# Two graph-attention layers on one core: VectorE in fixed order at the joint of the layers, and the first half tile's shift read from PSUM

## The chip, the cores and the metric

The kernel runs on one core of a Trainium2 chip. A core has five engines with a queue each: TensorE (PE; its weight loads are listed apart as PEld), VectorE (DVE), ScalarE (ACT), GpSimd (POOL) and SyncE (SP), which only issues transfers. The metric is the device time of one execution in microseconds; the time of a kernel is the median of its runs.

## The reference

Two layers, each with a residual, on x (2708 x 1024, float32) and a 0/1 adjacency matrix (2708 x 2708):

```
h = relu(layernorm(x))
layer 0:  f = h@Wf + bf;  g = h@Wg + bg
          e = relu(f @ g.T);   scores = where(adj > 0, e, -9e15)
          x = x + softmax(scores, axis=1) @ (h@W + bW)
h = relu(layernorm(x))
layer 1:  hh = h@W1;  f1 = hh@a1;  f2 = hh@a2
          e = leaky_relu(f1 + f2.T, 0.2);   scores = where(adj > 0, e, -9e15)
          x = x + relu(softmax(scores, axis=1) @ hh)
```

In layer 1 the scores are cheap: a column plus a row. The two vectors are computed as h@(W1@a1) and h@(W1@a2), that is, two dot products for each row of h.

## The kernel before, in words

The nodes are cut into 22 tiles of up to 128 (128 partitions) and into 5 panels of four tiles each (three panels have a few columns more). Tiles are taken in pairs; NQ = 10 pairs and one left-over unit. All large products are done by one level of Strassen's scheme (products M1 to M7, on halves); layer 1's panels 1 to 4 use two levels in the aggregation.

Layer 0 goes panel by panel: scores, softmax, `aggregate` (weights times h), `project` (times W). After `project` of a tile, `rows_done` has the new rows of x: it normalizes them into h, takes the two dot products (`dots(0)` into f[0], which is f1, `dots(1)` into f[1], which is f2) and raises the running column maximum of masked f2 for every panel (`raise_max`). `pair_h` forms Strassen sums of the pair's h (tiles g) and stores them.

The joint of the layers begins when the last panel (tiles 16 to 19, pairs 8 and 9) is projected. For a tile of that panel `rows_done` takes dots(1) at once, raises panel 0's maximum, and appends dots(0) to a list. After the last tile, `shifts1(0, make)` turns the running maximum (mx) by five TensorE transposes (mx_ps in `column_max`), reduces it to the columns mcol, and makes three small columns in some eight VectorE instructions: z, "none" and the shift m. Between the transposes and the reductions it calls `make`, the first half of `pair_h`; the second half, `rest[0]`, follows.

Then `take_weights(0)` calls `weights1(0, ...)`. For panel 0 the unnormalized scores of eight tiles were made ahead (`scores_before`, tiles P). `spread` puts the shift column along a row on all partitions: TensorE transposes into a PSUM bank sp_ps (four columns to a bank), and `copy` moves that to mb, by VectorE and ScalarE in turns. For each of the eight tiles the shift mb is then subtracted and ScalarE takes the exponential; for the others, two more spreads (of z and "none", into ub and vb) come first. `aggregate(1, 0, ...)` follows: its first product M1 reads the left half (288 columns) of the first tile, into the banks gx.

What sets the order. The program's text gives an order of tracing; a planner then orders each engine's instructions when the kernel is built. An instruction that is ready goes before one that is not; among ready ones the earlier in the program goes first. `tc.keep_in_program_order` ties an instruction behind the one traced before it on its engine. `InOrder` applies that to every instruction of the engines named in `nc.hold`; here `nc.hold` is empty. Loads by SyncE always keep program order. Deferred work stands in the list `later` with a price in us; `behind(us)` adds credit and runs entries while there is credit (in layer 1's panel 0, 4.0 at each call, four calls in a product), the loads of the first entries being issued ahead. `weights1` puts its 24 entries (2.1 each) before those already listed; running maxima for the panels 2 to 4 stand in a second list, `lazy`, which is used when `later` is empty.

All tiles named h_last, P, mb, maskl, g and most others come from one pool of 54 buffers of 128 x 576 float32; hc (rows of h for the aggregation) from a pool of 12.

Of the kernel before, what the change touches and what calls it, by code (L numbers as in the profile page):

```python
# [11 lines left out]
AF = mybir.ActivationFunctionType  # L12
# [45 lines left out]
def kernel(  # L58
# [19 lines left out]
    nc = InOrder(tc)  # L78
# [31 lines left out]
    NQ = len(pairs)  # L110
    pair_of = {t: (t // 2, t % 2) for t in range(MONO)}
    LEFT = NQ
    units = pairs + [(MONO, TINY)]
# [11 lines left out]
    def slot(name, shape=(P, WX), dt=FP):  # L125
        return slots.tile(list(shape), dt, tag="slot", name=name)
# [18 lines left out]
    def bank(name, shape=(P, W), dt=FP):  # L145
        return psum.tile(list(shape), dt, tag="bank", name=name)
# [44 lines left out]
    def copy(o, i):  # L191

        flip[0] ^= 1
        (nc.vector.tensor_copy if flip[0] else nc.scalar.copy)(o, i)
# [6 lines left out]
    def put(us, go, fetch=None, takes_psum=False, ready=None, to=later):  # L201
        to.append([us, fetch, go, takes_psum, ready])

    def one(of=None):
        of = later if of is None else of
        for it in of[:4 if of is lazy and from_slots[0] else ahead[0]]:
            if it[1]:
                it[1]()
                it[1] = None
        us, _, go = of.pop(0)[:3]  # L210
        go()
        return us

    def behind(us, psum_free=False):
# [3 lines left out]
        while spare[0] and not later and lazy and credit[0] > 0:  # L218
            credit[0] -= one(lazy)

    def flush():
        while later:
            one()
# [18 lines left out]
    def halves(t):  # L242
        return [t[:, e * W:(e + 1) * W] for e in range(2)]
# [1 line left out]
    def row_halves(name, from_stream=False):  # L245
        return halves(stream(name)) if from_stream else [slot(name)[:, :W] for _ in range(2)]

    def spread(o, cols):

        at = 0  # L250
        for g in range(0, len(cols), 4):
            ps = bank("sp_ps")
            w = 0
            for cl in cols[g:g + 4]:
                n = cl.shape[0]
                nc.tensor.transpose(ps[:, w:w + n], cl.to_broadcast([n, P]), ident[:n, :n])
                w += n
            copy(o[:, at:at + w], ps[:, :w])
            at += w

# [14 lines left out]
    def sub(o, a, b):  # L275
        nc.vector.tensor_tensor(o, a, b, OP.subtract)

    def columns_of(p, col):
        return [col[:n, i:i + 1] for i, (_, n) in enumerate(pieces[p])]
# [357 lines left out]
    for name, gs in (("pick_lo", (0, 1)), ("pick_hi", (0, 2, 3))):  # L637
        t = consts.tile([P, P], FP, name=name)
        cols = lambda g: ident[:, B32 * g:B32 * (g + 1)]
# [667 lines left out]
    f = [consts.tile([P, n], FP, name=f"f{k}") for k, n in enumerate((NCOL, NT))]  # L1307
# [204 lines left out]
    def shifts1(p, between=None):  # L1512

        k, t0 = len(pieces[p]), first_col[p]
        top = column_max(p, mx[p], between)[:, :k]
        f1 = f[0][:, t0:t0 + k]
        z, m, c, d = (stats.tile([P, 5], FP, name=nm)[:, :k] for nm in ("z", "m1", "none", "m2"))
        nc.vector.tensor_add(z, f1, top)
        nc.vector.tensor_scalar(c, top, -BIG / 2, None, op0=OP.is_ge)
        nc.vector.tensor_scalar(d, top, -BIG / 2, -BIG, op0=OP.is_lt, op1=OP.mult)  # L1520
        nc.vector.scalar_tensor_tensor(m, z, ALPHA, z, op0=OP.mult, op1=OP.max)
        nc.vector.tensor_mul(m, m, c)
        nc.vector.tensor_add(m, m, d)
        sub(z, f1, m)
        nc.vector.scalar_tensor_tensor(c, f1, ALPHA, m, op0=OP.mult, op1=OP.subtract)
        return z, c, m
# [3 lines left out]
    def rows_done(t, xt):  # L1530

        done_rows[t] = xt

        def dots(k):
            c = t if k else col_of[t]
            dot(f[k][:, c:c + 1], done_rows[t], halves(wab[k]))
            if k == 1:
                nc.vector.tensor_scalar(f2s[:, t:t + 1], f[1][:, t:t + 1], ALPHA, None, op0=OP.mult)
            elif t == MONO:
                nc.gpsimd.dma_start(f[0][:NM, HALF:HALF + 1], f[0][NM:, c:c + 1])  # L1540

        q, k = pair_of.get(t, (LEFT, t - MONO))
        mine = units[q]
        whole = all(s in done_rows for s in mine)
        if panel_of[t] == NP - 1:
            done_rows[t] = row_halves("h_last")
            normalize(xt, done_rows[t])
            if whole and q == NQ - 1:
                tc.keep_in_program_order(nc.scalar.activation(stats.tile([P, 1], FP, name="warm"), eps, AF.Exp))
            raise_it = lambda: raise_max(0, q, k, first_mask[t][:, :width[0]])  # L1550
            if not whole:
                dots(1)
                raise_later.append(raise_it)
                put(1.6, lambda: dots(0))
            else:
                raise_later.pop()()
                dots(1)
                raise_it()
                put(1.6, lambda: dots(0))
                rest = []  # L1560
                make = lambda: rest.append(pair_h(q, *(done_rows[s] for s in pairs[q])))
                if q == NQ - 1:
                    got["zm"] = shifts1(0, make)
                else:
                    make()
                rest[0]()
                put_max(1, q)
                if q == NQ - 1:
                    for m in BY_QUARTERS:
                        put_quarters(m, q // 2, later)  # L1570
                    for p in range(2, NP):
                        for s in (NQ - 2, NQ - 1):
                            put_max(p, s, lazy)
            return

        def met():
            known.add(q)
            for p in range(NP):
                if generated[p] > q:
                    put_max(p, q)  # L1580
        put(1.5, lambda: moments(xt))
        put(0.5, lambda: normalize(xt))
        put(1.6, lambda: dots(0))
        put(1.6, lambda: dots(1))
        if whole and q == LEFT:
            put(0.0, lambda: left_h(1, *(done_rows[s] for s in mine)))
            put(0.0, met)
        elif whole:
            put(2.7, lambda: pair_h(q, *(done_rows[s] for s in pairs[q])))
            put(0.0, met)  # L1590
            quads_met[q // 2] = quads_met.get(q // 2, 0) + 1
            if quads_met[q // 2] == 2:
                put(0.0, lambda: [put_quarters(m, q // 2) for m in BY_QUARTERS])
# [82 lines left out]
    got = {}  # L1676
    generated = [0] * NP
    before, spreaded = {}, []
# [27 lines left out]
    for p in range(NP):  # L1706
# [3 lines left out]
        S = got["S"]  # L1710
# [34 lines left out]
    def weights1(p, z, m, shift):  # L1745

        w = width[p]
        ub, vb1, sm = slot("ub"), slot("vb1"), slot("sm")

        def spreads():  # L1750
            spread(ub, columns_of(p, z))
            spread(vb1, columns_of(p, m))
        if p == 0:
            mb = slot("mb")
            spread(mb, columns_of(p, shift))
        else:
            spreads()
        S = [None] * NT
        order = order_of_units
        exps[0] = 0  # L1760

        def go(i, mk):
            if i < len(order):
                q, k = order[i]
                n, t = P, units[q][k]
                if p == 0 and t in before:
                    S[t] = before.pop(t)
                    s = S[t][:n, :w]
                    sub(s, s, mb[:n, :w])
                else:  # L1770
                    if p == 0 and not spreaded:
                        spreads()
                        spreaded.append(True)
                    S[t] = slot("P")
                    s = S[t][:n, :w]
                    nc.scalar.activation(s, vb1[:n, :w], AF.Identity, bias=f2s[:n, t:t + 1])
                    nc.vector.scalar_tensor_tensor(s, ub[:n, :w], f[1][:n, t:t + 1], s, op0=OP.add, op1=OP.max)
                    add(s, s, mk[0][:n, :w])
                nc.scalar.activation(s, s, AF.Exp)
            if i >= LAG:  # L1780
                q, k = order[i - LAG]
                total(p, sm, S[units[q][k]], once(q, k), i == LAG)
            exps[0] += 1

        front = []
        for i in range(len(order) + LAG):
            mk = []
            front.append([2.1, (lambda i=i, mk=mk: mk.append(load_mask(p, *order[i])))
                          if i < len(order) and not (p == 0 and units[order[i][0]][order[i][1]] in before) else None,
                          (lambda i=i, mk=mk: go(i, mk)), False, None])  # L1790
        later[:0] = front
        return S, sm
# [39 lines left out]
    for p in range(NP):  # L1832
        S, sm = got["P"]
# [5 lines left out]
        g = aggregate_quartered(p, S, sm, next_right, then, fine=1.0) if p else aggregate(1, p, S, sm, then, rate=4.0)  # L1839
# [34 lines left out]
```

## Time and profile before

| | |
|---|---|
| median of 3 runs | 3078.0 us (3077.63 to 3078.73) |
| the profiled execution | 3082.24 us, span 3080.5 us |
| TensorE busy | 3000.0 us, 97% |
| VectorE busy | 2046.6 us, 66% |
| ScalarE, GpSimd busy | 551.7 us, 505.5 us |
| last product of layer 0 ends | 2124.9 us |
| transposes of the running maximum | 2133.19 to 2134.52 us |
| transposes of the shift, z and "none" | 2138.37 to 2142.47 us |
| first product of layer 1 | 2142.53 us |

The span runs from the first to the last instruction of the program; what lies around it is in the execution's time. Times in rows are microseconds from the start of the span. Almost all VectorE and ScalarE work has line 45, a helper's, so it is told apart by the names of tiles: "mx<-maskl,f,mx" is `raise_max`, "junk<-h_last,wab" a pass of a dot product (two for each), "f<-part" the sum of the two passes, "g<-h_last" a sum of `pair_h`, "mcol<-mx_ps" a reduction, "P<-P,mb" the subtraction of the shift.

### The profile page before, as it was taken

How to read it: one execution, taken by the hardware profiler on the slowest of the kernel's cores; microseconds unless marked ns; L12 is line 12 of the kernel's file. 1: busy time of each engine (PE TensorE's matmuls, PEld its weight loads, DVE VectorE, ACT ScalarE, POOL GpSimd, SP SyncE). 2: the span in 40 equal slices, each digit the busy share in tenths (PEclk: the TensorE clock that was granted, in tenths of full speed). 3: DMA queues.
4: the chain of work that ended last, by engine and by line, in shares of the span. 5: the costliest groups of instructions: out<-in, count | busy, mean ns of one | idle time of the engine just before them, and what ended most of it. 6: DMA issues, size and time to landing. Idle time of an engine off the chain costs nothing.

```text
span 3080.5 us, 41669 instructions
## 1 busy us (share of the span) xinstructions
PE 3000.0 (97%) x14630; PEld 2301.1 (75%) x14630; DVE 2046.6 (66%) x4577; ACT 551.7 (18%) x895; POOL 505.5 (16%) x786
## 2 busy tenths in 40 slices
PE   8998999899999999999999999998999999999998
PEld 4576777657877588885888886784767959879695
DVE  5776693776661586715965276867878768787853
ACT  3420020021110121101211011302222131212200
POOL 1421101310011110214102011131202010020202
PEclk9999999999999999999999999998999999999999
DMA  6988967987565786758967588679757768878786
GB/s 220 304 259 245 302 248 251 314 285 228 177 241 146 226 262 218 247 155 240 284 206 253 165 233 275 230 292 323 250 193 266 260 203 295 289 268 297 266 293 249
DMA packets 447809, 766.80 MB, mean 249 GB/s; under 512 B 175488, under 2 KB 262304, under 8 KB 447568
## 3 DMA queue, kind: packets, MB, share of 16 engines
q1 hardware_dynamic: 392624, 598.30, 60.1%
q0 software_dynamic: 54976, 165.83, 16.1%
q8 instruction: 116, 1.90, 0.2%
q14 instruction: 93, 0.76, 0.1%
HBM read 630.04 MB, written 138.11 MB: 249 GB/s over the span
## 4 chain that ended last, share of the span: by engine, by line
PE 79%; DVE 9%; DMA 5%; issue 5%; SPq 1%; ACT 1%; POOL 0%; POOLq 0%; DVEq 0%; ACTq 0%
PE sz L1385 7%; PE gz L664 6%; PE gx L664 6%; PE gy L664 6%; PE gz L1074 5%; PE pz L1274 5%; PE sx L1385 5%; PE px L1274 4%; PE sy L1385 4%; PE py L1274 4%; PE gx L1074 3%; PE gy L1074 3%; PE gv L664 3%; PE M_ps L577 3%; PE qz L664 3%
## 5 line engine op out<-in xcount | busy, mean ns | idle before, releaser
L1385 PE MATMUL sz<-B,As 128*128 128x288 f32 (+2 forms) x1200 | 292.7, 393 | 3.4 <-DVE st L45 3.3
L1385 PEld LDWEIGHTS sz<-B,As 128*128 128x128 f32 x1200 | 228.1, 191 | 53.0 <-DVE st L45 6.8
L1385 PE MATMUL sx<-B,As 128*128 128x288 f32 (+2 forms) x800 | 203.0, 397 | 13.5 <-DMA As<-hs_d 12.0
L1385 PE MATMUL sy<-B,As 128*128 128x288 f32 (+2 forms) x800 | 199.0, 392 | 0.0
L664 PE MATMUL gz<-Sa,hc 128*128 128x288 f32 (+2 forms) x800 | 190.3, 399 | 6.3 <-DMA hc<-hg_d 6.3
L1385 PEld LDWEIGHTS sx<-B,As 128*128 128x128 f32 x800 | 153.4, 192 | 47.5 <-DMA As<-hs_d 8.0
L664 PEld LDWEIGHTS gz<-Sa,hc 128*128 128x128 f32 x800 | 154.5, 194 | 40.4 <-DMA hc<-hg_d 6.7
L1385 PEld LDWEIGHTS sy<-B,As 128*128 128x128 f32 x800 | 151.7, 190 | 30.6 <-DVE st L45 0.3
L1074 PE MATMUL gz<-quarter,hc 128*128 128x128 f32 (+2 forms) x1344 | 168.8, 279 | 3.8 <-DVE gT L45 3.7
L143 POOL DMA_DIRECT2D out_dram<-x_res x180 | 89.1, 501 | 482.0 <-DVE x_res L45 473.5
L1074 PEld LDWEIGHTS gz<-quarter,hc 128*128 128x128 f32 x1344 | 160.6, 191 | 5.1 <-DVE gT L45 4.6
L1274 PE MATMUL px<-w,gT 128*128 128x512 f32 x320 | 141.2, 593 | 1.5 <-ACT pt L45 1.5
L1274 PE MATMUL py<-w,ps 128*128 128x512 f32 x320 | 142.2, 593 | 0.0
L1274 PE MATMUL pz<-w,ps 128*128 128x512 f32 x320 | 142.1, 594 | 0.0
L143 POOL DMA_DIRECT2D mk_d<-mask x55 | 36.0, 654 | 523.7 <-DVE mask L45 517.3
L1274 PEld LDWEIGHTS pz<-w,ps 128*128 128x128 f32 x320 | 60.2, 190 | 76.2 <-issue 70.5
L1274 PEld LDWEIGHTS py<-w,ps 128*128 128x128 f32 x320 | 60.5, 190 | 75.1 <-issue 72.7
L1274 PEld LDWEIGHTS px<-w,gT 128*128 128x128 f32 x320 | 60.1, 190 | 72.9 <-issue 67.1
L577 PE MATMUL M_ps<-wgT,wfT 128*128 128x512 f32 x256 | 112.5, 595 | 1.6 <-ACT hsT L45 1.6
L664 PE MATMUL gy<-T,hc 128*128 128x288 f32 (+2 forms) x480 | 111.6, 394 | 0.0
L45 ACT ACTIVATE P<-P 128x576 f32<-128x576 f32 (+2 forms) x110 | 72.0, 655 | 207.5 <-DVE P L45 207.4
L984 POOL TENSOR_TENSOR gT<-gT,rr 128x2304 f32<-128x2304 f32 (+5 forms) x12 | 44.4, 3700 | 378.0 <-DVE rr L45 172.7
(382 smaller groups left out, 5892.1 us busy)
## 6 DMA issues: line engine op xcount, KB each, us to landing
hc<-hg_d SPq DMA_DIRECT2D x175, 512.0 KB
As<-hs_d SPq DMA_DIRECT2D x150, 512.0 KB
hc<-hr_d SPq DMA_DIRECT2D x119, 512.0 KB
hc<-hs_d SPq DMA_DIRECT2D x112, 512.0 KB
w<-wt_d SPq DMA_DIRECT2D x96, 512.0 KB
w<-in_L_gnn_W_dram SPq DMA_DIRECT2D x72, 512.0 KB
md<-md_d SPq DMA_DIRECT2D x56, 512.0 KB
adj_i<-in_adj_dram SPq DMA_DIRECT2D x200, 128.0 KB
```

What stands on the lines that cost most here:

```text
L45: i = f(*a, **k)
L143: nc.gpsimd.dma_start(a, b)
L577: nc.tensor.matmul(ps, wfT[a][c // NH][:, c % NH, :], wgT[b][c], start=(c == 0), stop=(c == NC - 1))
L664: nc.tensor.matmul(ps[d], left(m, k, d), right(m, k), start=(start and k == 0), stop=(k == K - 1), skip_group_check=True)
L984: nc.gpsimd.tensor_tensor(of(e, s), of(e, s), by(s, k), OP.mult)
L1074: nc.tensor.matmul(ps[:, d], lhs[:, d * P:(d + 1) * P], inner_right(m, n, k), start=(start and k == 0 and d == 0), stop=(k == NK - 1), ski ...
L1274: nc.tensor.matmul(ps, left[i][m][:, k, :], w_[k], start=(start and k == 0), stop=(k == NH - 1), skip_group_check=True)
L1385: nc.tensor.matmul(ps[:n, :h], lefts[q][:, i % 2, c, :n], B[m][c // 2][:, c % 2, :h], start=(start and c == 0), stop=(c == NH - 1), skip_g ...
```

## The change

- Two helpers: `held(f, ...)` runs f with VectorE's instructions tied to program order; `call` runs it plainly.
- `rows_done`, last panel: dots(0) of the tiles of pair 8 is done at once instead of being listed; that of pair 9 stays listed and is held. For pair 9 the last `raise_max`, `shifts1` with the first half of `pair_h`, and the second half are held.
- `weights1`, panel 0: the spread of the shift is held, and `sooner` is called when the first four transposes are issued: it subtracts the shift from the first half of the first tile straight from the PSUM bank and takes the exponential of that half. The first tile's entry then does the second half alone; the subtractions of the first three tiles are held.

```diff
+    def held(f, *a):
+        was, nc.hold = nc.hold, ("vector",)
+        r = f(*a)
+        nc.hold = was
+        return r
+
+    def call(f, *a):
+        return f(*a)
...
-    def spread(o, cols):
+    def spread(o, cols, sooner=None):
...
+            if sooner and g == 0:
+                sooner(ps)
             copy(o[:, at:at + w], ps[:, :w])
...
             if not whole:
                 dots(1)
                 raise_later.append(raise_it)
-                put(1.6, lambda: dots(0))
+                dots0 = lambda: dots(0)
+                if q == NQ - 1:
+                    put(1.6, lambda: held(dots0))
+                else:
+                    dots0()
             else:
+                last = q == NQ - 1
                 raise_later.pop()()
                 dots(1)
-                raise_it()
-                put(1.6, lambda: dots(0))
+                (held if last else call)(raise_it)
+                if last:
+                    put(1.6, lambda: held(dots, 0))
+                else:
+                    dots(0)
                 rest = []
                 make = lambda: rest.append(pair_h(q, *(done_rows[s] for s in pairs[q])))
-                if q == NQ - 1:
-                    got["zm"] = shifts1(0, make)
+                if last:
+                    got["zm"] = held(shifts1, 0, make)
                 else:
                     make()
-                rest[0]()
+                (held if last else call)(rest[0])
                 put_max(1, q)
...
         if p == 0:
             mb = slot("mb")
-            spread(mb, columns_of(p, shift))
+            t = units[0][0]
+
+            def sooner(ps):
+                s = before[t][:, :w // 2]
+                sub(s, s, ps[:, :w // 2])
+                nc.scalar.activation(s, s, AF.Exp)
+            held(spread, mb, columns_of(p, shift), sooner)
         else:
             spreads()
...
                 if p == 0 and t in before:
                     S[t] = before.pop(t)
-                    s = S[t][:n, :w]
-                    sub(s, s, mb[:n, :w])
+                    s = S[t][:n, (w // 2 if i == 0 else 0):w]
+                    (held if i < 3 else call)(sub, s, s, mb[:n, (w // 2 if i == 0 else 0):w])
```

## The prediction

> **What bounds the kernel now.** I read the page first, then TensorE's waits from 2075 us on, the chain, the timeline of the joint engine by engine, and SyncE's waits there. The page:
>
> ```profile
> span 3080.5 us, 41669 instructions
> PE 3000.0 (97%) x14630; PEld 2301.1 (75%) x14630; DVE 2046.6 (66%) x4577; ACT 551.7 (18%) x895; POOL 505.5 (16%) x786
> ```
>
> TensorE is busy 97% of the span, so a gain elsewhere counts only where TensorE stands still. Its waits between 2075 us and the end, longest first:
>
> ```profile
> PE mx_ps L856 <- DVE mx L45: 8.3, 1, 8.3
> PE gz L1089 <- DVE V L45: 4.6, 3, 2.2
> PE sp_ps L256 <- DVE m L45: 4.4, 2, 3.9
> ```
>
> The first row and 3.85 us of the third are the joint of the layers: TensorE ends layer 0 at 2124.9, transposes the maximum at 2133.19, the shifts at 2138.37, and starts layer 1 at 2142.53. The chain there (start, duration, work) runs through VectorE:
>
> ```profile
> 2131.06 0.60 DVE g L45
> ...
> 2131.74 0.61 DVE junk L45 x2
> ...
> 2132.41 0.72 DVE mx L45
> 2133.14 0.60 DVE g L45
> 2133.74 0.61 DVE junk L45 x2
> 2134.35 0.60 DVE g L45
> 2134.95 0.98 DVE mcol L45 x5
> 2135.94 0.60 DVE g L45
> ...
> 2136.89 0.61 DVE junk L45 x2
> ...
> 2137.59 0.64 DVE junk L45 x2
> ...
> 2142.53 21.25 PE gx L664 x80
> ```
>
> "mx" is the last running maximum, "mcol" the five reductions. "g" (sums for Strassen) and "junk" (dot products) are needed by nobody here: they were ready while the chain's next instruction was not, and then the chain waited for them. TensorE's own timeline:
>
> ```profile
> 2138.37 1.41 PE L256 MATMUL sp_ps<-ident,m 128*128 128x128 f32 x5 [3.85 <-DVE m L45]
> 2139.72 1.41 PE L256 MATMUL sp_ps<-ident,z 128*128 128x128 f32 x5
> 2141.06 1.41 PE L256 MATMUL sp_ps<-ident,none 128*128 128x128 f32 x5
> 2142.53 17.86 PE L664 MATMUL gx<-P,hc 128*128 128x288 f32 x66
> ```
>
> These 15 transposes run without a gap and end 0.06 us before the first product. So the product has two releasers that come almost together: the exponential (the chain's view) and TensorE's own three groups.
>
> **The skill.** "TensorE: Matmul & The Clock Gate", section "What's actually happening", says that the clock is halved after an idle window of about 3.4 us and returns after about 3.4 us of sustained work, on a free-running window. The trace agrees: the granted clock is 0.50 in every slice from 2130 to 2144, 1.00 from 2146; the first 80 products take 21.25 us, the next 80 19.40, so the cold start costs 1.85 us. "PSUM — Partial Sum Buffer", section "Engine vs sequencer instructions", says that VectorE's queue is strictly first in, first out and that matmuls start in program order; that is what makes fillers and transposes binding, and the timeline shows nothing against it. "VectorE: DVE Perf Modes", section "Why PSUM operands drop a tier", says that fp32 operands in PSUM run at the base rate; here a 128x288 subtraction takes 459 ns from SBUF (T<-P) and 435 to 458 ns for an addition from PSUM (m<-gy, gT<-gy), so reading PSUM costs nothing extra.
>
> **Part 1: the dots of tiles 16 and 17 are traced at once.** Each is two 0.61 us passes and a small sum, 2.6 us for both tiles. They leave the joint, where they were fillers, and land between 2101 and 2112. VectorE idles there (0.88 at 2104.6, 1.65 at 2112.1, 3.27 at 2116.4), so they are absorbed before 2119.7. At most they delay the eviction of py at 2110.20 by about 2.6 us, to 2113.5; its bank is needed at 2114.4. Cost zero; without the cover, under 1 us.
>
> **Part 2: the last maximum.** Before, one g and one junk pass lie between the accumulator read (end 2131.06) and mx (2132.33). With the sums and the dots of tiles 18 and 19 held behind, nothing ready is left; the scalar f, its scaled copy and mx follow with waits of about 0.04 us between dependent instructions (as at 2123.55 and 2123.75): f 2131.10, copy 2131.28, mx 2131.36. Gain 0.97; mx ends 2132.17.
>
> **Part 3: maximum to reductions.** Before: g, junk, g, 1.81 us. After: the two held sums, the second dependent on the first: 0.61 + 0.72 = 1.33; the transposes need about 1.15 beside them. Gain 0.48.
>
> **Part 4: reductions to the shift.** The g at 2135.94 (0.60) moves behind the small instructions. The two junk passes and the f between them (0.61 + 0.07 + 0.64) go too; the small instructions, which overlap them now, then show their own latency, about 0.3. Gain 0.60 + 1.32 - 0.3 = 1.6. Parts 2 to 4 give 3.0: the shifts' transposes start at 2135.4 in place of 2138.37.
>
> **Part 5: the first half straight from PSUM.** After the shift VectorE issues the last two sums (1.3 us) beside the first four transposes (1.1), then a 128x288 subtraction (0.45) and ScalarE an exponential (0.40 as for the 128x288 copy m<-qx): ready about 2.3 us after the transposes start. It takes the full copy (0.60), half a subtraction (0.30) and half an exponential (0.29) off that branch, 1.2 us. But the other two groups of transposes stand before the product in the program, they are ready at once, and 15 of them last 4.1 us at the half clock. So the branch has 1.8 us of slack and this part gives only the 0.06. The second half costs one more small instruction on VectorE and on ScalarE, under 0.2 us, beside two products of TensorE (over 3 us cold).
>
> **Part 6: dots of tiles 18 and 19.** They move behind the weights, 2.6 us of VectorE near 2190 to 2197. That queue is full until 2205 (39.90 of 40 us from 2165 to 2205), but starts 3 us earlier and has lost two dot passes (2140.4, 2151.9). The next TensorE needs there, sums for the product at 2205 and the bank of gy (2224), were done by 2193 and 2196. Cost zero; without the cover at most 2.6.
>
> **Part 7: what moves in the queues.** The list of deferred work loses two entries of 1.6 us. With 4.0 us of credit at each call, the first four mask loads of the later panels' maxima are then issued before, not after, the first two loads of the third-next product (M6, first used 2205.25). And four buffers (h_last of tiles 18 and 19) stay taken from about 2141 or 2152 until about 2195. SyncE is a queue in order and does wait for such buffers:
>
> ```profile
> SPq L139 <- DVE P L45: 22.2, 5, 11.7
> SPq L139 <- DVE junk L45: 12.4, 2, 8.4
> ```
>
> Before, M6's first two loads were issued by 2168.1 and six masks then held the queue from there to 2195.3. Behind the masks, M6's loads would be issued near 2192 (3 us earlier, as VectorE's work is) and land some 5 us later (estimate from 3.9 for a 256 KB load of the same tensor and 5.4 for a 512 KB store to it): 2197 against a need at 2202. Hidden, with 5 us of cover instead of over 30.
>
> **Sum.** 0.97 + 0.48 + 1.6 + 0.06 = 3.1, less about 0.1 for the extra small instructions: 3.0. The clock's phase can move this: before, the product started just after a window began and was cold for 3.2 us; another phase costs up to one window more, 1.7 us, or saves a few tenths. I take zero, since the runs shown contain such phases too. TensorE is busy nearly without a break afterwards (368.3 of 385 us from 2095 to 2480; of the 16.7 missing, 12.1 lie between 2125 and 2143), so the 3.0 carries to the end. The profiled execution took 3082.24 (span 3080.5); this would make its span 3077.5. The median of the runs, 3078.0, lies 4.2 lower than the profiled execution; I subtract the same difference: **3075.0 us**.
>
> **Rivals.** 0.2% of the time is 6.2 us; a measurement of this kernel can hardly tell less from no change, so a move from 3071.8 to 3084.2 is "same".
>
> B, the product goes ahead of the two other groups of transposes: then part 5 counts and 1.8 more is won: 3073.2. For it: the product would be ready then. Against: they come earlier in the program, are ready earlier, and stood first before.
>
> C, the fixed order doesn't shorten the chain, or another filler (a running maximum of panel 1, 0.73 each) takes the place of the dots, or the clock warms a window later, or a later wait takes the gain: 3077 to 3080. For it: only named instructions are held, others may still slip in. Against: no running maximum ran between 2133 and 2193.
>
> D, slower: part 7 goes wrong. The four buffers and the earlier masks hold SyncE, M6's loads come late and TensorE stands at the start of M6. It decides for "slower" from a stall of 9.2 us (3.0 + 6.2) on; that needs the loads issued 14 us after my 2192, at 2206. For it: SyncE already waited up to 11.7 us at once for VectorE there. Against: VectorE frees the buffers of the maxima and masks from 2193 to 2198. With 10 to 12 us of stall the time is 3085 to 3087.
>
> E, the new plan orders later panels better as well and takes most of the 6.5 us of short waits for V, gT and pt: about 3071. Nothing in the diff aims at them.
>
> **Numbers.** A (as forecast, 3073.8 to 3076.5) 0.54; B 0.10; C 0.17; D 0.14, of which 0.12 above 3084.2 and 0.02 between 3080 and it; E 0.05. The range 3072.8 to 3081.0 takes in A, B, C and the clock's phase and leaves out E and most of D. Faster 0.05 (E), same 0.83 (A, B, C and the rest of D), slower 0.12.
>
> **What would show it.** TensorE's wait for mx falls from 8.3 to about 7.3, that for m from 3.85 to about 1.8; the product starts near 2139.5, still right behind fifteen transposes without a gap (else B); no junk or g between mx and mcol but two sums; the 128x288 subtraction from sp_ps ends over 1.5 us before the product. D would show as a wait of gz for hc. I am wrong if a filler is back in the chain, if the transposes are reordered, or if a wait for DMA appears after 2195.

## The result: slower by 5 us, and the joint shorter as forecast

| | before | after |
|---|---|---|
| median, side by side on one chip (12 runs each) | 3080.16 us (3076.93 to 3084.51) | 3086.15 us (3081.28 to 3090.86) |
| the profiled execution | 3082.24 us, span 3080.5 us | 3086.87 us, span 3085.1 us |

The ratio is 1.0017, 95% interval 1.001 to 1.0024: slower by 0.1 to 0.24%, some 5 us. Forecast were 3075.0 us and a gain of 3. The range of the kernel before is wider here than the three runs suggested on which the forecast stood, so below only ratios to the kernel before on the same chip are compared. In the code after the change the rows of before stand 9 to 11 lines lower: L664 (the aggregation's products) is L675, L256 (spread) L265, L856 (column maximum) L867.

Page of the changed kernel, span and busy time:

```profile
span 3085.1 us, 41670 instructions
PE 3005.3 (97%) x14630; PEld 2303.8 (75%) x14630; DVE 2048.4 (66%) x4578; ACT 551.4 (18%) x896; POOL 504.0 (16%) x786
```

The number of matmuls is the same, and TensorE is busy 5.3 us longer: part of the loss is work at a lower clock, not standing still. TensorE's waits from 2075 us on (total, times, longest):

```profile
PE mx_ps L867 <- DVE mx L45: 7.7, 1, 7.7
PE gz L1100 <- DVE V L45: 4.5, 3, 2.2
PE gz L1085 <- DVE gT L45: 3.7, 3, 1.4
PE gz L675 <- DMA hc<-hr_d: 3.4, 1, 3.4
PE sp_ps L265 <- DVE m L45: 2.3, 2, 1.8
```

The waits of the joint fell (mx 8.3 to 7.7, the first wait for m 3.85 to 1.8). New is the fourth row: M6 (into gz) waits once, 3.4 us, for a tile of h. TensorE's timeline from the joint to the product after M6 (start, duration, count, wait ahead of it):

```profile
2135.36 1.41 PE L265 MATMUL sp_ps<-ident,m 128*128 128x128 f32 x5 [1.81 <-DVE m L45]
2136.70 1.41 PE L265 MATMUL sp_ps<-ident,z 128*128 128x128 f32 x5
...
2139.38 22.23 PE L675 MATMUL gx<-P,hc 128*128 128x288 f32 x80
...
2203.08 11.80 PE L675 MATMUL gz<-P,hc 128*128 128x288 f32 x48
2218.29 9.69 PE L675 MATMUL gz<-P,hc 128*128 128x288 f32 x32 [3.41 <-DMA hc<-hr_d]
2227.82 15.68 PE L675 MATMUL gy<-P,hc 128*128 128x288 f32 x64
```

And the kernel before in the same place:

```profile
2205.25 19.56 PE L664 MATMUL gz<-P,hc 128*128 128x288 f32 x80
2224.65 15.68 PE L664 MATMUL gy<-P,hc 128*128 128x288 f32 x64
```

The account, start against start. The shifts' transposes begin 3.0 us earlier than before (2135.36 against 2138.37), the first product 3.15. M6 begins 2.17 earlier: the first 80 products took 22.06 us in place of 21.09, because the clock stayed at half longer. M6 itself takes 24.74 us in place of 19.40: 3.41 of standing still and 1.93 more, of which about 1.7 is the clock, halved again from 2219.7 for 3.4 us. The next product starts 3.17 late. The end is 4.6 late, and what was added on the way is again the clock: after a wait of 2.2 us for VectorE (the row for V), which both kernels have, it was at half for 6.8 us from 2462.0, where before it was so for 3.4 us from 2459.8. The changed kernel's lateness grows there from 3.1 to 4.5 us.

What TensorE waited for stands in SyncE's queue. The changed kernel (issue time, total of the stretch, number of transfers):

```profile
2189.09 4.19 SPq L139 DMA_DIRECT2D maskl<-mk_d  x4
2193.33 0.98 SPq L139 DMA_DIRECT2D hc<-hr_d  x2
2194.41 7.35 SPq L139 DMA_DIRECT2D maskl<-mk_d  x6
2201.81 0.43 SPq L139 DMA_DIRECT2D hc<-hr_d  x1
2202.33 6.52 SPq L139 DMA_DIRECT2D maskl<-mk_d  x2
2208.91 10.53 SPq L139 DMA_DIRECT2D hc<-hr_d  x6
```

The kernel before:

```profile
2177.27 18.03 SPq L139 DMA_DIRECT2D maskl<-mk_d  x6
2195.35 0.42 SPq L139 DMA_DIRECT2D hc<-hr_d  x1
2196.28 8.06 SPq L139 DMA_DIRECT2D maskl<-mk_d  x5
2204.39 0.43 SPq L139 DMA_DIRECT2D hc<-hr_d  x1
2209.40 0.32 SPq L139 DMA_DIRECT2D maskl<-mk_d  x1
```

A load of hc is 512 KB and feeds 16 matmuls, so M6's 80 need five loads; the fourth is needed 48 matmuls, 11.64 us, after M6 starts. Before, two loads went out by 2168, then six masks, the third load (2195.35), five masks, the fourth load (2204.39), the last mask (2209.40). After: four masks, two loads, six masks, the third load (2201.81), two masks, and only then the fourth load (2208.91). It has changed places with the last mask, and that mask waits. SyncE's waits from 2180 to 2212 in the changed kernel:

```profile
SPq L139 <- DVE junk L45: 23.4, 2, 20.9
SPq L139 <- DMA hs_d<-hq: 9.8, 2, 5.6
```

The second row is the wait of the last masks: their buffers are those of quarter sums (hq, sums of quarters of h for the later panels), which first have to be stored. The first row, 20.9 us at a stretch, is the wait of the first mask for buffers which the held dots ("junk") give back late.

### The profile page after: what moved, and what is told of

It reads as the page before. It is cut to its first block, busy times and chain, and to the rows that moved or that the text cites. A ratio compares the mean times of both kernels' runs of the same rounds, so it can differ in the third digit from the quotient of the medians.

```text
span 3085.1 us, 41670 instructions
## 1 busy us (share of the span) xinstructions
PE 3005.3 (97%) x14630; PEld 2303.8 (75%) x14630; DVE 2048.4 (66%) x4578; ACT 551.4 (18%) x896; POOL 504.0 (16%) x786
## 4 chain that ended last, share of the span: by engine, by line
PE 76%; DVE 11%; DMA 6%; issue 4%; SPq 1%; ACT 1%; POOL 1%; DVEq 0%; POOLq 0%; ACTq 0%
PE sz L1396 7%; PE gx L675 6%; PE gy L675 6%; PE gz L1085 5%; PE gz L675 5%; PE sx L1396 5%; PE sy L1396 4%; PE pz L1285 4%; PE px L1285 4%; PE qz L675 4%; PE py L1285 3%; PE gx L1085 3%; PE gy L1085 3%; PE gv L675 3%; PE M_ps L588 3%
## 5 line engine op out<-in xcount | busy, mean ns | idle before, releaser
L675 PE MATMUL gz<-Sa,hc 128*128 128x288 f32 (+2 forms) x800 | 190.5, 399 | 6.4 <-DMA hc<-hg_d 6.4
L675 PEld LDWEIGHTS gz<-Sa,hc 128*128 128x128 f32 x800 | 154.6, 194 | 40.6 <-DMA hc<-hg_d 6.9
L675 PE MATMUL gy<-T,hc 128*128 128x288 f32 (+2 forms) x480 | 111.6, 394 | 0.0
L45 ACT ACTIVATE P<-P 128x576 f32<-128x576 f32 (+3 forms) x111 | 72.1, 650 | 206.6 <-DVE P L45 206.5
```

Of the source, the lines that this page charges most:

```text
L45: i = f(*a, **k)
L675: nc.tensor.matmul(ps[d], left(m, k, d), right(m, k), start=(start and k == 0), stop=(k == K - 1), skip_group_check=True)
```

## The experiments

**The theory** after reading these views: with two entries fewer in the deferred list, M6's fourth load stands behind the last mask, and that order makes it late. **Rivals:** the buffers of h of tiles 18 and 19, kept until about 2193 by the held dots, make it late whatever the order; or the shorter joint alone does, because M6 starts earlier against a queue that does not. All ratios are to the kernel before on the same chip.

**Two empty entries put back.** The changed kernel, with the list as long as before:

```diff
                 else:
                     dots0()
+                    put(1.6, lambda: None)
...
                 else:
                     dots(0)
+                    put(1.6, lambda: None)
```

> The changed kernel with two empty entries of 1.6 us put where the dots of tiles 16 and 17 stood in the deferred list, so that mask loads and hc loads stand in SyncE's queue as before. Theory Q (queue order: the list is two entries shorter, so masks stand ahead of M6's loads): no wait of gz for hc, the first product of layer 1 still near 2139.4, so about 3 us faster than before (3 of joint, give or take 1.7 for the phase of the clock) and about 8 faster than the change. Theory B (buffers: h_last of tiles 18 and 19 held until about 2193): the wait of gz for hc stays at 2 to 4 us and the time is that of the change, 4 to 6 us above before.

Measured: 3084.12 us, ratio 0.9998 (0.999 to 1.0007). The fourth load is ahead of the last mask again and in time; a wait of 0.4 is left, for M6's fifth load. The product starts 4.02 us after the first transpose of the shifts, as in the changed kernel. So the loss goes away with the order, while the dots of 18 and 19 are still held and the joint is still short. The gain of 3 does not show in the interval.

**The dots of tiles 18 and 19 listed, but not held.**

```diff
-                    put(1.6, lambda: held(dots0))
+                    put(1.6, dots0)
...
-                    put(1.6, lambda: held(dots, 0))
+                    put(1.6, lambda: dots(0))
```

> The changed kernel, but the listed dots of tiles 18 and 19 are not tied to program order, so that they can run early and free their four buffers; the list stays two entries shorter. Theory Q: M6's fourth load still stands behind all twelve masks, gz waits 2 to 4 us for hc, the time is 2 to 6 us above before. Theory B: buffers come free near 2145, the wait goes away, 2 to 3 us faster than before. Both: those dots may fill in at the joint again, up to 1 us.

Measured: 3084.52 us, 1.0002 (0.9994 to 1.0011). The dots slip into the joint again; TensorE's waits there:

```profile
PE mx_ps L867 <- DVE mx L45: 8.2, 1, 8.2
PE sp_ps L265 <- DVE mcol L45: 3.3, 1, 3.3
```

From layer 0's last matmul to the first product it takes 17.43 us (before 18.27, after 15.41). The order in SyncE's queue is the changed kernel's, but M6 loses only some 0.3 us; theory Q's wait of 2 to 4 us did not come. So holding is what makes the joint shorter, and the order alone did not bring the whole stall.

**The kernel before, with the dots of tiles 16 and 17 at once** and nothing else changed:

```diff
-                put(1.6, lambda: dots(0))
+                if q == NQ - 1:
+                    put(1.6, lambda: dots(0))
+                else:
+                    dots(0)
```

> The kernel before with one part of the change alone: the dots of tiles 16 and 17 at once. Theory Q: M6's loads come late though nothing is held, gz waits 2 to 4 us for hc and the clock is halved for a window, 3 to 6 us slower than before, less about 1 us for the fillers that have left the joint. Theory B: no wait of gz for hc, since all h_last buffers come free early; 0 to 2 us faster than before.

Measured: 3084.15 us, 1.0000 (0.9992 to 1.0008). This one part brings the changed kernel's order in the queue; the fourth load is issued 3.98 us after M6's start and M6 takes 20.0 us. It costs 0.6 us at M6, within the noise. Theory Q missed here too; the forecast of theory B fits.

**Two empty entries, and the first tile's shift whole, from SBUF.** As the first experiment, without the half tile from PSUM:

```diff
-            held(spread, mb, columns_of(p, shift), sooner)
+            held(spread, mb, columns_of(p, shift))
...
-                    s = S[t][:n, (w // 2 if i == 0 else 0):w]
+                    s = S[t][:n, :w]
```

> As the version with two empty entries, but without the half tile from PSUM: the whole first tile is shifted from mb, as before. My step 5 (the fifteen transposes bind): the first product starts within 0.3 us of the same place, 4.0 us after the first shift transpose, and the time is the same within 0.2%. The rival (the half tile matters): the product starts 1 to 1.5 us later, behind the exponential of the whole tile.

Measured: 3082.22 us, 0.9991 (0.9985 to 0.9998). TensorE's timeline:

```profile
2134.64 1.41 PE L265 MATMUL sp_ps<-ident,m 128*128 128x128 f32 x5 [1.81 <-DVE m L45]
...
2138.66 21.66 PE L675 MATMUL gx<-P,hc 128*128 128x288 f32 x80
```

The product starts 4.02 us after the first transpose, with the half tile from PSUM or without it: that part of the change is worth nothing here.

**The changed kernel again,** unedited.

> The changed kernel again, beside the versions below on one chip. If the late load is a property of its order and buffers, gz waits for hc again by 2 to 4 us at the seventh pair of M6 and M6 takes 22 to 25 us in place of 19.4; the time is 3 to 6 us above before. If the first profile caught an accident, M6 takes under 20.5 us and the time is within 2 us of before.

Measured: 3088.36 us, 1.0024 (1.0013 to 1.0034). The wait for hc is 4.7 us and the clock is halved for 6.8 us; M6 takes 27.02 us.

**The product ahead of ten of the transposes.** The first experiment, and pairs 8 and 9's tiles are begun only behind the first products, so that the transposes of z and "none" come after them:

```diff
-        exps_until(NQ)
-        for q in range(NQ):
+        early = NQ - 2 if l else NQ
+        exps_until(early)
+        for q in range(early):
...
+        def rest_of_first():
+            exps_until(NQ)
+            for q in range(early, NQ):
+                sub(t1(q), wa_(q)[:, hi], wa_(q)[:, lo])
...
+                                    **({(M1, NQ // 2): rest_of_first} if l else {}),
```

> As the version with two empty entries, with the tiles of pairs 8 and 9 begun behind the first products of layer 1, so that the ten transposes of z and none stand behind them in the program. My rival B: the first product starts 1.8 us sooner, near 2.3 us after the first shift transpose in place of 4.0, and the ten transposes run later, partly at full clock: 1 to 2 us faster than the version with empty entries. If the cold clock simply lasts longer by that much (it returns at the end of a window with products in it), up to half of that is given back.

Measured: 3082.58 us, 0.9998 (0.999 to 1.0006). TensorE's timeline:

```profile
2137.94 1.41 PE L265 MATMUL sp_ps<-ident,m 128*128 128x128 f32 x5 [1.81 <-DVE m L45]
2140.25 8.56 PE L675 MATMUL gx<-P,hc 128*128 128x288 f32 x24 [0.90 <-ACT P L45]
2148.65 0.80 PE L265 MATMUL sp_ps<-ident,z 128*128 128x128 f32 x5
```

The product starts 2.31 us after the first transpose, 1.71 sooner than in the first experiment. But the transposes are still TensorE's to do: from the first transpose to M6 it takes 67.54 us, against 67.39 there, though the clock stayed halved 1.2 us less of that time. The work was moved, not taken away.

**The dots of tiles 18 and 19 taken early, four empty entries.** The changed kernel, but the two dots run ahead of the weights' list, on a VectorE that is not yet full:

```diff
-                    put(1.6, lambda: held(dots0))
+                    joint_dots.append(dots0)
+                    put(1.6, lambda: None)
                 else:
                     dots0()
+                    put(1.6, lambda: None)
...
+        if p == 0:
+            front[8:8] = [[1.6, None, (lambda d=d: held(d)), False, None] for d in joint_dots]
```

(and the same for the dots of the second tile of each pair)

> As the version with two empty entries, but the dots of tiles 18 and 19 stand behind the eighth tile's weights instead of at the end of the list, which holds four empty entries: the queue's order is that of before and the four buffers come free near 2150. If both causes count, no wait of gz for hc at all (0.4 us remained with empty entries alone) and the start of the product stays 2.9 us earlier than before, counted from the end of layer 0: 2 to 3 us faster than before. If only the order counts, the same as the version with empty entries.

Measured: 3081.62 us, 0.9989 (0.9981 to 0.9998): faster than before, if only just. The wait for hc is 0.5 us, for the fifth load, so freeing the buffers early did not take away the 0.4 us that was left. That it is faster than the version with empty entries alone is not shown; the intervals overlap.

**Both of the last two together,** the edits as shown.

> Both of the two versions before this one together: products ahead of the ten transposes, early dots, empty entries. Expected 3 to 5 us faster than before (2.9 from the chain, 1.8 from the transposes, less what the clock's phase takes), and no wait of gz for hc. If the transposes' place doesn't matter, 2 to 3 us faster.

Measured: 3084.25 us, 1.0005 (0.9995 to 1.0015), not the gain expected. In the first product TensorE waits for exponentials (gx for P) twice: 0.9 us at its start, as in the version without early dots, and 1.9 us more inside it, which is more than the 1.7 that the transposes' place was to win.

**All of M6's loads ahead of the masks.** The changed kernel, whole, with one edit:

```diff
-        spare[0] = p < 2
+        spare[0] = p == 1
+        if p == 0:
+            then[M6] = lambda: spare.__setitem__(0, True)
```

> The changed kernel whole, with one edit: the list of the second layer's late mask loads is opened only when M6 of its first panel ends, so that every h tile of M6 is ahead of all twelve masks in SyncE's queue. Nothing else moves. Theory of the queue (M6's fourth load stands behind the last mask, and the joint itself is about 2.8 us shorter): no wait of M6 for h, M6 19.4 to 19.7 us, and 2 to 3 us faster than the kernel before (ratio 0.999). Rival, buffers (the loads are late because the dots hold the buffers, wherever the masks stand): a wait of 2 us or more stays in M6, 3084 to 3088. Rival, the masks are now too late themselves: a wait for a mask in the second layer's panels, slower by more than 5 us.

Measured: 3083.34 us, 0.9995 (0.9986 to 1.0004). SyncE's timeline, where M6's five loads are among the eight, and then TensorE's:

```profile
2168.92 16.18 SPq L139 DMA_DIRECT2D hc<-hr_d  x8
2191.53 20.66 SPq L139 DMA_DIRECT2D maskl<-mk_d  x12
```

```profile
2202.91 19.56 PE L675 MATMUL gz<-P,hc 128*128 128x288 f32 x80
```

No stall, and M6 takes 19.40 us to the start of the next product, with the short joint and the held dots of the changed kernel. The held buffers, in this order, do no harm. A gain of 2 to 3 us is neither shown nor excluded by the interval.

**The list four entries shorter.** The dots of 18 and 19 taken early as above, with no empty entry, so the buffers come free early and still more masks stand ahead:

```diff
-                    put(1.6, lambda: held(dots0))
+                    joint_dots.append(dots0)
...
-                    put(1.6, lambda: held(dots, 0))
+                    joint_dots.append(lambda: dots(0))
```

(and the lines that put them ahead of the weights' list)

> The changed kernel with the dots of tiles 18 and 19 taken ahead of the product too, on the idle VectorE, and no entry put in their place: the list is four entries shorter than before, and the buffers of 18 and 19 come free early. Theory of the order: nine masks now stand ahead of M6's first two loads in SyncE's queue, these are issued at 2198 to 2204, and M6 waits 3 to 8 us for h in its first pairs; slower than the kernel before by 2 to 8 us although the buffers are free. Rival, buffers alone: with the dots done early there is no wait for h, and it is 2 to 3 us faster than the kernel before.

Measured: 3093.26 us, 1.0026 (1.0016 to 1.0036). SyncE's timeline, and then TensorE's:

```profile
2185.40 17.91 SPq L139 DMA_DIRECT2D maskl<-mk_d  x9
2203.36 0.98 SPq L139 DMA_DIRECT2D hc<-hr_d  x2
2209.46 3.78 SPq L139 DMA_DIRECT2D maskl<-mk_d  x3
2213.29 13.80 SPq L139 DMA_DIRECT2D hc<-hr_d  x7
```

```profile
2208.63 7.92 PE L675 MATMUL gz<-P,hc 128*128 128x288 f32 x32
2224.02 13.53 PE L675 MATMUL gz<-P,hc 128*128 128x288 f32 x48 [7.47 <-DMA hc<-hr_d]
```

Now nine masks are ahead of M6's first two loads, as expected at 2203; these still come in time, though the first is issued only 5.3 us before M6. The third stands behind the last mask and costs 7.47 us. Free buffers do not prevent the stall; the order makes it.

**The early dots without the half tile from PSUM,** as the faster version above with the edit of the fourth experiment.

> As the kernel with the early dots and four empty entries (3081.62, 1.6 us under the kernel before), but the whole tiles' shift comes from the buffer in SBUF as before, without the half tile from PSUM. If the half tile is worth nothing, as forecast: the product starts 4.0 us after the first transpose of the shifts, and the time is the same as with it, 1.5 to 3 us faster than the kernel before (ratio 0.999). If it is worth its 0.3 us or more: the product starts 4.3 us or later after the first transpose.

Measured: 3083.71 us, 0.9994 (0.9987 to 1.0001); the product starts 4.03 us after the first transpose. The half tile is worth nothing again.

**The changed kernel's order, the buffers free.** The early dots with two empty entries in place of four; the SyncE order is that of the changed kernel, load by load.

```diff
                 else:
                     dots0()
-                    put(1.6, lambda: None)
```

(against the faster version; the same for the second tile)

> The kernel with the early dots of tiles 18 and 19, but with two empty entries in place of four: they stand for these two dots alone, so the deferred list has the length of the changed kernel's and SyncE issues its masks and h tiles in exactly the changed kernel's order. The joint and the product's start are the changed kernel's. What differs is only that the four buffers of h of tiles 18 and 19 come free some 40 us earlier. If the order alone makes the stall: the fourth load of M6 is issued 5 to 6.5 us after M6's start as in the changed kernel, a wait of gz for hc of 3 us or more and a halved clock follow, ratio to the kernel before 1.001 to 1.003. If the order and the held buffers are both needed: the fourth load is issued 4 us or less after M6's start, the wait is under 0.7 us, and the time is 1 to 3 us under the kernel before.

Measured: 3082.85 us, 0.9998 (0.999 to 1.0006), and neither answer holds as written. The fourth load is late (5.56 us after M6's start), which was the answer "order"; the wait is 1.8 us, in the middle, and the clock is not halved. SyncE's timeline, and then TensorE's:

```profile
2177.89 11.71 SPq L139 DMA_DIRECT2D maskl<-mk_d  x4
2189.65 1.80 SPq L139 DMA_DIRECT2D hc<-hr_d  x2
2191.56 8.90 SPq L139 DMA_DIRECT2D maskl<-mk_d  x6
2200.51 0.43 SPq L139 DMA_DIRECT2D hc<-hr_d  x1
2201.03 6.10 SPq L139 DMA_DIRECT2D maskl<-mk_d  x2
2207.18 10.45 SPq L139 DMA_DIRECT2D hc<-hr_d  x6
```

```profile
2215.19 8.00 PE L675 MATMUL gz<-P,hc 128*128 128x288 f32 x32 [1.76 <-DMA hc<-hr_d]
```

**All together.** The times are us after layer 0's last matmul started (2124.26 before, 2123.97 after). "Needed" is M6's start plus 11.64; "used" is when the matmul ran.

| kernel | order | dots 18, 19 | first product | 4th load issued | needed | used | M6 takes |
|---|---|---|---|---|---|---|---|
| before | load ahead of last mask | loose | 18.27 | 80.13 | 92.63 | in time | 19.40 |
| two empty entries | load ahead | held | 15.40 | 79.73 | 90.41 | in time | 20.05 |
| early dots, four entries | load ahead | early | 15.41 | 78.89 | 90.46 | in time | 20.12 |
| before, dots of 16, 17 at once | load behind | loose | 18.43 | 84.63 | 92.29 | 92.73 | 20.00 |
| not held | load behind | loose | 17.43 | 83.84 | 91.61 | 91.87 | 19.73 |
| early dots, two entries | load behind | early | 15.42 | 83.91 | 89.99 | 91.92 | 21.40 |
| after | load behind | held | 15.41 | 84.94 | 90.75 | 94.32 | 24.74 |
| after, again | load behind | held | 15.42 | 84.14 | 89.31 | 94.15 | 27.02 |

Three terms can be read off it.

- The order moves the issue of the fourth load from about 80 to about 84 to 85, because it goes behind a mask that waits for the store of a quarter sum. That time hardly depends on the joint: with a joint of 18.4 it is 84.6, with 15.4 it is 83.9 to 84.9.
- The shorter joint moves the need from 91.6 to 92.6 down to 89.3 to 90.8. In the two rows with the new order and a longer joint, the matmul runs 0.3 to 0.4 after the need (where 16 and 17 alone were changed, the profile puts the 0.28 us down to a running maximum, not to the load); with a short joint and the buffers free it runs 1.9 after it.
- The held dots move the arrival from about 92 to 94.2: the load takes 9.4 and 10.0 us from issue to use in the two rows of the changed kernel, and 8.0 to 8.1 in the three rows where the buffers come free early. The first masks go out at 65.1 in the changed kernel, at 54.6 with the early dots, so traffic is pressed into less time. The two kernels from 2195 to 2205 (busy time by engine, then the clock, the DMA share and GB/s), first the changed one:

```profile
2195.00:2205.00 10.00, 10.00 (x47) 7.36 (x46) 8.97 (x22) 1.60 (x4) 6.08 (x9) 1.00 0.89 291
```

and with the early dots and two entries:

```profile
2195.00:2205.00 10.00, 10.00 (x47) 7.36 (x46) 8.46 (x23) 1.59 (x4) 7.37 (x11) 1.00 0.73 228
```

The first two terms are shown by runs that change one of them. For the third, that the buffers matter is shown; that the pressed traffic is the means is argued from these rows, not tried by itself. From 2205 to 2215 both are full (a DMA share of 1.02 and of 1.05), so it could only be what had piled up before.

The five kernels that keep the short joint and put the fourth load in time without moving transposes (two empty entries with and without the half tile, early dots with and without it, all loads ahead of the masks) stand at 0.9998, 0.9991, 0.9989, 0.9994 and 0.9995, on average 2.0 us faster than before. Two of these intervals leave out 1. The profiles show it with less scatter if they are counted from layer 0's last matmul, which started anywhere from 2118.1 to 2133.7 us: from there to the end of the span it is 956.2 us before, 961.1 and 961.9 in the two profiles of the changed kernel, and 952.2 to 954.6 in these five.

## Why the prediction was wrong

**Parts 2 to 4, right,** though it is luck that the figures agree so closely. The forecast put the shifts' transposes at 2135.4; they started at 2135.36. But layer 0's last matmul started 0.29 us earlier in this profile, at 2123.97, and the wait for mx fell to 7.7, not to the 7.3 forecast. Counted from that matmul the transposes start 2.7 us sooner than before, where 3.0 was forecast. VectorE's timeline of the changed kernel:

```profile
2131.36 0.81 DVE L45 SCALAR_TENSOR_TENSOR mx<-maskl,f,mx 128x576 f32<-128x576 bf16 x1
2132.10 0.68 DVE L45 TENSOR_TENSOR g<-h_last 128x512 f32<-128x512 f32 x1
...
2133.42 1.06 DVE L45 TENSOR_REDUCE mcol<-mx_ps 128x1 f32<-128x128 f32 x5
...
2136.70 0.45 DVE L45 TENSOR_TENSOR P<-P,sp_ps 128x288 f32<-128x288 f32 x1
```

The maximum started at the forecast 2131.36; only two sums lie between it and the reductions (the second, at 2132.81, is left out here), and the other two stand behind the small instructions, ahead of the half tile's subtraction.

**Part 5, right.** The half tile's exponential was done at 2137.62, 1.76 us before the product (forecast: 1.8 of slack), and fifteen transposes without a gap set the start. Of two pairs of kernels with and without the part, one is a little faster without it (0.9998 and 0.9991) and one with it (0.9989 and 0.9994), with overlapping intervals; the product's start is the same in all four, 4.02 to 4.03 us after the first transpose.

**Part 1, right by itself.** Alone in the kernel before, it costs nothing that can be measured (1.0000). But it is what takes two entries out of the list, which is Part 7.

**Part 6** got the dots' place right (2188.4 to 2193.7), and no wait of TensorE for VectorE came of them at M6. That they keep four buffers until then is in Part 7.

**Part 7 is the step that failed**: "M6's loads would be issued near 2192 ... and land some 5 us later ...: 2197 against a need at 2202. Hidden, with 5 us of cover instead of over 30." For the first two loads this came true: issued at 2193.33 and 2193.8, no wait at M6's start. But M6 has five loads and the list twelve masks, and I followed the order only as far as the first two. The fourth load, not the first, had lost its cover: it had gone behind the last mask. Three of that step's terms were wrong there:

- "3 us earlier, as VectorE's work is." VectorE was full from 2165 to 2205. Holding its fillers back from the joint postpones them, it doesn't remove them. The first quarter sums, whose stores free the last masks' buffers, start at 2198.12 before and 2196.82 after, only 1.3 us earlier. TensorE was moved up against a queue that was not.
- "Some 5 us later". From 2205 to 2215 the DMA share is 1.02, and the fourth load took 9.4 us from issue to use.
- The stall of 3.41 us was followed by a halved clock, and that took some 1.7 more. The forecast priced no second cold start.

**The sum's last step** failed with it: "so the 3.0 carries to the end". A TensorE that is busy without a break before the change shows only that nothing comes late at the old times.

**Rival D** was the right mechanism in the wrong place: it put the stall at M6's start, and from there asked for loads issued at 2206. At the fourth load 4 to 5 us later in the queue, with a need some 2 us earlier, were enough. Its time of 3085 to 3087 was met by luck: it stood for a stall of 10 to 12 us on top of 3075.0; what came was 3.4 us of stall, more time at the half clock, and a kernel before that measured 3080.16, not 3078.0. **Rival B** was wrong in its price: a product ahead of ten transposes starts 1.7 us sooner and M6 starts no sooner. Of **rival C**, the longer cold start came, at 1.0 us in this profile; in the second profile of the changed kernel the first 80 products took 20.61 us, 0.5 less than before, so it is not a property of the change. The cold start before, which the forecast gave as 1.85 us, is 1.69 from start to start (21.09 against 19.40).

## What to carry to other kernels

When an edit makes a list of deferred work shorter or longer, write out the whole new order of the load queue to the last deferred item, and give each later load its own time of need: the one that loses its cover need not be the next one. A gain on TensorE is paid out only if the loads and buffers of the stages behind it move up with it; those that hung on a full VectorE, on stores or on a full DMA moved up much less here, or not at all. Work that is held out of a critical chain comes due later, with the buffers that it keeps.

## What was not expected of the hardware

**The clock's phase is a term of its own.** From the first transpose of the shifts to M6's start all these kernels have 15 transposes and 256 matmuls of products. In the twelve profiles without moved transposes TensorE works through this stretch with hardly a wait. It takes 66.27 us plus half of what the clock stays halved beyond 6.3 us after the first transpose, within 0.02 us, or 0.07 for the kernel before. So it is 66.27 at 6.3 us (after, again), 66.88 at 7.4 (before), 67.39 at 8.6 (two empty entries) and 67.72 at 9.2 (after). The changed kernel itself has two of these values: one program, and 1.45 us between two profiles of it.

**What halves the clock.** The Trainium skill, "TensorE: Matmul & The Clock Gate", section "What's actually happening", gives an idle window of about 3.4 us, free-running. The runs agree only in part. A wait of 1.76 us left the clock at 1.00, one of 3.41 was followed by half a clock for 3.4 us, and waits of 4.68 and 7.47 by half a clock for 6.8 us each. But in all fourteen profiles TensorE also waits 2.2 us for V, ending between 2451 and 2471 us. After that wait the clock was at half for 3.4 us in eight of them, for 6.8 us in four (both of the changed kernel among these) and not at all in two. So a wait of 2.2 us can be enough, and the same wait need not be; what else decides is open. After the joint's long pause the clock was at half for 13.7 or 17.1 us in all of these kernels. In the twelve profiles above it came back only 5.9 to 9.2 us after the first of the shifts' transposes, although TensorE worked from there with hardly a wait.
